# Start-up of a planned attention layer: the second group's input loaded first, one query buffer cleared at once, the first group's normalisation given to VectorE

## The chip, the cores and the metric

The program runs on one core of a Trainium2 chip. Its metric is device time in microseconds, the median of several executions. A profiled execution adds a trace: every instruction of the five engines (TensorE, shown as PE with its weight loads as PEld; VectorE as DVE; ScalarE as ACT; GpSimd as POOL; SyncE as SP, which here only issues transfers) with start, duration and what it waited for.

## The reference, cut to what matters

Two transformer layers over x of 2 x 2048 x 256. Each computes a layer norm, then adds an attention and a mixture of experts of the same normalised x. Layer 0, which the change is about, is:

```python
xn = layernorm(x)                                  # 4096 rows of 256
q = rope((xn @ Wqa @ Wqb)  -> 16 heads of 16)
k, v = (xn @ Wkva @ Wkvb)  -> 4 heads of 16, k = rope(k)
w = softmax(causal(q k^T / 4)); out = (w v) @ Wout + bout
logits = xn @ Wg                                   # 8 experts, top 2, capacity 1280
y = sum over the 2 experts of gate * (gelu(a) * g) @ W_out,  [a, g] = xn @ W_in
x = x + out + y
```

Layer 1 has an attention with 32 fixed keys and sparsemax, and a second mixture of experts. Nothing of it is edited.

## The kernel before, in words

**Tiles.** The 4096 rows are eight *groups* of 512 rows (4 tiles of 128), four per batch. A group is fetched into one of two buffers `xg`, normalised in place, turned (`normed`, tile `tp`, result `xnT` in a ring of two `xt`), multiplied with the joined low-rank and gate weights (`lows`, tile `lw`, result `low`), and its gate logits are turned back (`logits`, tile `tpl`). From `low` come keys and queries of a 512-row block: `rope_products` (tile `pab`) multiplies twice, VectorE multiplies by the cosine and sine tables `cs_sb`, a sum makes the rotated value, ScalarE rounds it (`rope_high`), a subtraction gives the rest (`rope_low`), and both parts go to DRAM (`kd`, `qd`) and come back spread over partitions into `ks` (5 buffers) and `q` (4 buffers). These buffers must be zero elsewhere: `clean_k` by ScalarE, `clean_q` by GpSimd. The tables come from `cs` products; the values from `make_v` (tile `pv`, weights `wkv16[64:96, 8:12]`).

**Attention.** A unit is one group of four heads over 512 queries, `j`. Its row maxima are found first: `maxima` (tile `s`, then VectorE's maximum `part`), `negate_max`, `flip_max` (`mtT`, `mr`), and `place_max`, which sends the maxima into `q`. Then `score` (tile `sc`, exponential on ScalarE into `es`) and `values` (tile `av`).

**Experts.** After all eight groups' logits, `p_route` chooses and counts (tile `before`), GpSimd scatters 4096 rows twice into `buf` (64 indirect transfers at L734), and six experts of layer 0 (`ext`, `exh`, `exy`) are woven into the rest of the attention.

**Order.** Engines execute in the order written. That order is made while the program is built: a planner holds a time for each engine (`T["PE"]`, `T["V"]` VectorE, `T["A"]` ScalarE, `T["G"]` GpSimd, `T["S"]` SyncE), a list of `jobs` with the time from which each is ready, and picks what TensorE does next by a price among candidates. `later(eng, duration, ready, f, then)` adds a job; `flush()` writes down the jobs that are due. Engine names `VL`, `AV` and `AVL` leave a choice: `VL` is VectorE, but held back while GpSimd's time is ahead; `AV` is ScalarE or VectorE, whichever is free sooner; `AVL` is the same with GpSimd's time counted against VectorE. Where the planner sees a gap on TensorE in the early part, `fill()` writes a product that is not used (tile `idle`). `prep` holds the groups, tables, keys, queries and values in order of their due progress; `GRP0` and `GRPN` set those of the groups, `T.update(...)` the engines' starting times, and the argument of `landed` the time at which a group's x is taken to be there. All of these are numbers of the plan, not of the chip. `pin` keeps an instruction at its place in the program.

**Names and lines.** The transfers of the start are L366 to L381, `clean_q` L358, called at L382 and L383; a group's fetch is `fetch` (L411), its normalisation `layernorm_steps` (L205 and L206 statistics, L213 to L217 roots, L224 to L233 Newton steps on VectorE or L228 to L236 on GpSimd, L240 the normalised tile by ScalarE, L242 by VectorE); products are recorded under L336, turns under L339, SyncE's transfers under L345, the cast of turned tiles under L425, table copies L409, `low` copies L441, the rotation's product L458, its sum L1014, its rounding L465, its rest L472, clearing of keys L363.

Of the kernel before, what the change touches and what calls it, by code (L numbers as in the profile page):

```python
# [11 lines left out]
F32 = mybir.dt.float32  # L12
# [11 lines left out]
P = 128  # L24
# [125 lines left out]
def moe_transformer_kernel(  # L150
# [142 lines left out]
    with ExitStack() as actx:  # L293
# [38 lines left out]
        def pin(ins):  # L332
            return tc.keep_in_program_order(ins)
# [23 lines left out]
        def clean_q(i):  # L357
            pin(G.memset(qsl[i].bitcast(F32), 0.0))  # L358
# [14 lines left out]
        pin(A.dma_start(wa_sb[:, :, 0:96], wa.rearrange("(c p) m -> p c m", p=P)))  # L373
        pin(A.dma_start(wa_sb[:, :, 96:96 + NE], wg.rearrange("(c p) m -> p c m", p=P)))
        raw = [agx[rows, c0:c1].rearrange("p (v c) -> p v c", c=16) for rows, c0, c1 in ((slice(0, 64), 1024, 1536), (slice(64, 96), 1024, 1152))]
        pin(SP.dma_start(raw[1], wkvb[:, 0:256].rearrange("k (v c) -> k v c", c=32)[..., 0:16]))
        pin(SP.dma_start(raw[0].rearrange("p (v t) c -> p v t c", v=2), wqb.rearrange("k v t (g c) -> k v (t g) c", g=4)[..., 0:16]))
        pin(SP.dma_start(wkv16[64:96, 8:12], wkvb[:, 256:320].rearrange("k (g c) -> k g c", c=16)))
        for h in range(2):
            pin(A.dma_start(trif[64 * h:64 * h + 64], cst[:, C_TRI:C_TRI + P].rearrange("(r p) m -> p r m", p=64)))  # L380
        pin(A.dma_start(cst_sb, cst))  # L381
        for i in range(3):  # L382
            clean_q(i)  # L383
        pin(G.memset(identh, 0.0))
        for h in range(2):
            for r in range(2):
# [22 lines left out]
            pin(A.copy(cs_sb[:, :, 512 * blk:512 * blk + 512], ps))  # L409

        def fetch(grp):  # L411
            if grp == 0:
                return
            st[grp]["x"] = xgp.tile([P, 4, E], F32, tag="xg", name="xg")
            for i in range(0, 4, 2):
                sdma(st[grp]["x"][:, i:i + 2], xv[:, 4 * grp + i:4 * grp + i + 2])
# [48 lines left out]
            pin(A.copy(hi, tt[:, 0]))  # L465
            return hi

        def rope_low(tt, r, hi):
            n = tt.shape[0]
            at = 2048 + 512 * r  # L470
            lo = scr[:n, at:at + 512].bitcast(F32R)
            pin(G.tensor_tensor(lo, tt[:, 0], hi.bitcast(F32), ALU.subtract))  # L472
            return lo

        kss, qs, vas = {}, {}, {}
# [376 lines left out]
        def flush():  # L852
            now, done = T["PE"], False
            for job in sorted(jobs, key=lambda z: z[:2]):
                rank, _, eng, dur, ready, f, then = job
                if ready > now or (eng == "S" and T["S"] > now + ISSUE):
                    continue
                if eng in ("VL", "AVL"):
                    held = T["G"]
                    if eng == "VL":  # L860
                        eng = "V"
                        if held > now + 300 and now < ready + 3000:
                            continue
                    else:
                        eng = "A" if T["A"] + 70 <= max(T["V"], held) else "V"
                        if T[eng] > now + 300:
                            continue
                        dur, g = dur[eng == "V"], f
                        f = lambda: g(eng)
                    if eng == "V":  # L870
                        ready = max(ready, held)
                elif eng == "AV":
                    eng = "A" if T["A"] <= T["V"] else "V"
                    if T[eng] > now + 300:
                        continue
                    dur, g = dur[eng == "V"], f
                    f = lambda: g(eng)
                elif eng == "V" and T["V"] > now + 300 and now < ready + 5000:
                    continue
                if eng in "AG" and rank > 1 and T[eng] > now:  # L880
                    continue
                jobs.remove(job)
                moved[0] = 0
                f()
                end = on(eng, dur, ready)
                if eng == "S":
                    end = max(end + LAND, shift(moved[0], end))
                if then:
                    then(end)
                done = True  # L890
            return done
# [52 lines left out]
        def start_fetch(grp):  # L944
            i = take(xg)
            st[grp]["xg"] = i

            def landed(t):
                x_ = st[grp]["x"]
                steps = layernorm_steps(atp, x_, mean_sb[:, 4 * grp:4 * grp + 4], rstd_sb[:, 4 * grp:4 * grp + 4], x_, pin, V if grp < 2 else G)  # L950
                first = 0 if grp == 0 else 1
                costs = [500] * 4 + [600, 1900 if grp < 2 else 3900] + [350] * 4

                def go(k, t):
                    if k == len(steps):
                        at["x", grp] = t
                        later("S", ISSUE, t + 1500, lambda: keep_rows(grp), lambda t: x_done(grp, t), 2)
                    else:
                        if k < 6:
                            later("G" if k == 5 and grp > 1 else "VL" if k == 4 else "V", costs[k], t, steps[k],  # L960
                                  lambda t: go(k + 1, t if 3 < k < 6 and grp > 1 else t - HOP), first)
                        else:
                            later("AVL", (510, 350), t, steps[k], lambda t: go(k + 1, t - HOP), first)
                go(0, t)
            if grp == 0:
                return landed(4300)
            later("S", 2 * ISSUE, 0, lambda: fetch(grp), landed, 2)

        def p_normed(grp):
# [29 lines left out]
        def rope(n, products, done):  # L999
# [6 lines left out]
            def summed(t):  # L1006
                def high(t):
                    def low_(t):
                        at[key] = t
                        done(box, 1, t)  # L1010
                    done(box, 0, t)
                    later("G", 1270, t, lambda: box.update(lo=rope_low(box["tt"], box["r"], box["hi"])), low_, 0)
                later("A", 610, t, lambda: box.update(hi=rope_high(box["tt"], box["r"])), high, 0)
            later("G", 1270, free2[-1], lambda: pin(G.tensor_tensor(box["tt"][:, 0], box["tt"][:, 0], box["tt"][:, 1], ALU.add)),  # L1014
                  summed, 0)

        def both(key, f):

# [86 lines left out]
        for s, j in enumerate(order):  # L1105
            b, qb = j // 16, j // 4 % 4
            first_use.setdefault(("k", b, qb), s)
            first_use.setdefault(("q", j // 2), s)
        LEAD, MOST, EXB, SWX, RUN, ALONE, JOIN, IDLE, GAIN, GRP0, GRPN, QK0, QKN, FILL, TAIL = 2.5, 20.0, 243.0, 215.8, 2, 62.2, 125.5, 72.4, 5092.0, 15.0, 5.5, 36.4, 2.7, 136.0, 11.8
        tab, made = set(), set()  # L1110
        natural = []

# [16 lines left out]
        for s, j in enumerate(order):  # L1129
# [4 lines left out]
                n_qk += 1  # L1134
            grp = 4 * b + qb
            if 0 < grp < 2:
                add_group(grp, d)

            def load_tab(qb=qb):
                cs16["ring", qb] = take(xt)  # L1140
# [291 lines left out]
                    p_project(bq, i0)  # L1432
                yield t - now + late, t, go

        T.update(S=3000, A=3600, G=8500, V=2500)
        prefetch()
        prefetch()

# [1 line left out]
        pin(G.tensor_scalar(zero[:, E:E + 1], meta[:, 0, 0, 0:1], float(NT), None, ALU.add))  # L1440
        for i in range(NKS):
            later("A", 2560, 2000 + 5000 * i, lambda i=i: clean_k(i), None, 2)
        for i in range(3, NQS):
            later("G", 2000, 30000, lambda i=i: clean_q(i), None, 2)
        later("S", 9 * ISSUE, 40000, load_out_weights, None, 2)
        later("S", ISSUE, 48000, lambda: sdma(x1[NT:NT + P], zero[:, 0:E]), None, 2)
        for grp in range(8):
# [1170 lines left out]
```

## Time and profile before

| what | value |
|---|---|
| runs shown | 1947.78 us median (1944.43 to 1949.24, 3 runs) |
| profiled execution | 1942.78 us, span of its trace 1941.0 us |
| busy in the span | PE 1868.6, DVE 1237.6, ACT 1023.5, POOL 667.2 us |
| first maxima product (`s`) | starts at 46.38 us |
| first score (`sc`) | 64.86 us |
| experts counted (`before`) | 217.39 us |
| first expert turn (`ext`) | 426.0 us |
| granted TensorE clock | 0.984 in the mean |

The times of the last rows but one are starts in the trace, counted from the span's start. The profiled execution is 5.0 us shorter than the median of the runs, so sums made in the trace are carried to the median as differences.

### The profile page before, as it was taken

Reading aid. Unit: us, or ns where it says so; the run is one execution under the profiler, and the core shown is the slowest. Engines: PE = TensorE matmul, PEld = TensorE weight load, DVE = VectorE, ACT = ScalarE, POOL = GpSimd, SP = SyncE. Lnnn points to the kernel's source line nnn. Section 1 sums busy time; section 2 is a strip of 40 time slices with the busy share of each in tenths; the row PEclk is TensorE's granted clock in tenths of the full one; section 3 lists DMA queues with packets and bytes.
Section 4 is the critical chain, followed back from the end, with each engine's and each line's share of the span. In section 5 each row is a group of like instructions: output and inputs, shape, how many; then the busy total and the mean of one; then the engine's idle time right before and its main releaser. Section 6 shows DMA issues by size and latency. Waiting matters only on the chain.

```text
span 1941.0 us, 29444 instructions
## 1 busy us (share of the span) xinstructions
PE 1868.6 (96%) x10804; PEld 1128.9 (58%) x10818; DVE 1237.6 (64%) x2541; ACT 1023.5 (53%) x1915; POOL 667.2 (34%) x857
## 2 busy tenths in 40 slices
PE   9999999999999999999999999999899899999996
PEld 5554444445656656665565566556466355578774
DVE  4775777677666664566666766763122759997275
ACT  5354344565656566666666666666511433344451
POOL 5232467631222222223122212223223018755651
PEclk8998999999999999999999999999999899999999
DMA  5446456530233224433222312210152302255538
GB/s 144 144 145 193 140 175 203 159 92 12 64 70 97 67 47 114 110 70 91 74 56 65 84 45 38 51 29 12 37 111 25 109 17 79 99 177 157 184 123 265
DMA packets 144012, 192.92 MB, mean 99 GB/s; under 512 B 17261, under 2 KB 122227, under 8 KB 143730
## 3 DMA queue, kind: packets, MB, share of 16 engines
q1 hardware_dynamic: 115538, 137.18, 23.4%
q0 software_dynamic: 27072, 53.08, 11.6%
q8 instruction: 89, 1.46, 0.3%
q10 hardware_dynamic: 1248, 0.67, 0.1%
q14 instruction: 65, 0.53, 0.1%
HBM read 102.44 MB, written 95.77 MB: 102 GB/s over the span
## 4 chain that ended last, share of the span: by engine, by line
PE 79%; DVE 8%; ACT 4%; issue 3%; POOL 2%; DMA 2%; SPq 0%; ACTq 0%; DVEq 0%; POOLq 0%
PE sc L336 17%; PE av L336 13%; PE s L336 11%; PE exh L336 9%; PE exy L336 5%; PE gu L142 4%; PE po L142 4%; DVE srt L142 3%; PE acc L142 2%; PE pab L336 2%; PE pz L142 2%; DVE part L548 2%; PE idle L336 2%; PE po L336 2%; ACT es L587 2%
## 5 line engine op out<-in xcount | busy, mean ns | idle before, releaser
L587 ACT ACTIVATE es<-sc 128x512 f32<-128x512 f32 (+3 forms) x1280 | 634.9, 531 | 473.0 <-PE sc L336 445.4
L548 DVE TENSOR_REDUCE part<-s 128x2 f32<-128x1024 f32 (+3 forms) x640 | 649.8, 1058 | 249.9 <-PE s L336 248.4
L336 PE MATMUL sc<-q,ks 128*128 128x512 f32 (+3 forms) x1280 | 527.7, 461 | 11.2 <-ACT es L587 8.6
L336 PEld LDWEIGHTS sc<-q,ks 128*128 128x128 f32 x1280 | 220.5, 190 | 171.2 <-ACT es L587 87.8
L336 PE MATMUL av<-es,va 128*32 128x512 f32 (+3 forms) x2560 | 279.3, 539 | 1.9 <-POOL es L589 1.9
L589 POOL TENSOR_SCALAR_AFFINE_SELECT es<-es 128x256 f32<-128x256 f32 x256 | 106.7, 419 | 452.1 <-ACT es L587 450.7
L336 PE MATMUL s<-ks,q 64*128 64x512 f32 (+3 forms) x1280 | 226.4, 423 | 7.4 <-DVE part L548 3.6
L336 PEld LDWEIGHTS s<-ks,q 64*128 64x128 f32 x1280 | 101.6, 186 | 168.9 <-DVE part L548 69.0
L336 PEld LDWEIGHTS av<-es,va 128*32 128x32 f32 x2560 | 64.3, 109 | 117.1 <-issue 98.7
L809 POOL DMA_INDIRECT x<-low,tox x54 | 85.2, 1578 | 136.0 <-issue 37.7
L785 POOL TENSOR_TENSOR agx<-agx 128x1024 f32<-128x1024 f32 (+1 forms) x24 | 52.3, 2180 | 221.0 <-ACT agx L781 221.0
L336 PE MATMUL exh<-cs_sb,low 128*128 128x256 f32 (+1 forms) x480 | 120.7, 360 | 0.0
L336 PE MATMUL exh<-cs_sb 128*128 128x256 f32 (+1 forms) x480 | 120.1, 360 | 0.0
L142 POOL DMA_INDIRECT buf<-xn,slot x64 | 82.7, 1291 | 99.6 <-DVE cmp L142 80.3
L777 DVE COPY agx<-exh 128x512 f32<-128x512 f32 (+1 forms) x91 | 58.5, 643 | 89.7 <-PE exh L336 88.0
L142 POOL DMA_INDIRECT oe<-xn,to x72 | 78.1, 1085 | 46.9 <-ACT xn L142 29.6
L336 PEld LDWEIGHTS exh<-cs_sb 128*128 128x128 f32 x480 | 84.8, 190 | 11.8 <-ACT agx L777 0.3
L336 PEld LDWEIGHTS exh<-cs_sb,low 128*128 128x128 f32 x480 | 84.3, 189 | 12.5 <-issue 0.4
L336 PE MATMUL idle<-ones 128*128 128x256 bf16 (+2 forms) x506 | 82.6, 289 | 1.2 <-POOL ones L184 1.2
L142 DVE TENSOR_TENSOR srt<-srt 128x512 f32<-128x512 f32 (+6 forms) x104 | 75.6, 768 | 3.4 <-ACT srt L142 1.3
L734 POOL DMA_INDIRECT buf<-xsr,idx_sb x64 | 63.6, 993 | 24.1 <-issue 9.1
L142 PE MATMUL gu<-xg,xn 128*128 128x256 f32 x288 | 66.3, 382 | 0.2
(321 smaller groups left out, 2517.5 us busy)
## 6 DMA issues: line engine op xcount, KB each, us to landing
q<-qd SPq DMA_DIRECT2D x128, 128.0 KB
buf<-zero SPq DMA_DIRECT2D x20, 516.0 KB
buf<-zero SPq DMA_DIRECT2D x20, 514.0 KB
xn<-buf SPq DMA_DIRECT2D x18, 514.0 KB
qd<-agx SPq DMA_DIRECT2D x32, 256.0 KB
xsr<-xnd SPq DMA_DIRECT2D x32, 256.0 KB
oe<-zero SPq DMA_DIRECT2D x16, 512.0 KB
xn<-oe SPq DMA_DIRECT2D x16, 512.0 KB
```

The costliest lines, as they stand in the source:

```text
L142: return lambda *a, **k: self.tc.keep_in_program_order(f(*a, **k))
L336: pin(PE.matmul(*args, **kw))
L548: pin(V.tensor_reduce(parts[j][:, i, 2 * pair:2 * pair + 2, kb], sc[:, :, :n], AX.X, ALU.max))
L587: pin(A.activation(es[:, g % 2, :n], sc[:, :n], AF.Exp, scale=0.25))
L589: pin(G.affine_select(es[:, :, 0:P], es[:, :, 0:P], pattern=[[0, 2], [1, P]], compare_op=ALU.is_ge, fill=0.0, base=0, channel_multiplier=-1))
L734: pin(G.indirect_dma_start(ways[(2 * ti + k) % 8], bass.IndirectOffsetOnAxis(ap=idx_sb[:, k, ti:ti + 1], axis=0), xsr[:, ti % 3, k], None, ...
L777: pin((A.copy if eng == "A" else V.tensor_copy)(ag[i % 2][:, :, f, 0:n], exs["ps"][:, :, 0:n]))
L785: pin(eng.tensor_tensor(a, a, g, ALU.mult))
L809: pin(G.indirect_dma_start(x1[:], bass.IndirectOffsetOnAxis(ap=exs["to", i][:, c:c + 1], axis=0), ysx[:, c], None, compute_op=ALU.add))
```

## The change

Group 1's x is loaded by two SyncE transfers right behind the tables, ahead of the key, value and query weights; the value weights move to ScalarE's queue. Only one query buffer is cleared at the start; the three others become GpSimd jobs of the plan. The roots of group 0 go to plain VectorE and its normalised tiles to whichever of ScalarE and VectorE is free sooner. The rotation's sum and rest may go to VectorE when the plan finds GpSimd later by more than `ROPEV`. The plan's starting times, the landing of groups 0 and 1 and the due progress of group 1 are set anew. All later instructions are placed by the same planner from these numbers, so the order of the whole of layer 0 is written anew.

```diff
@@ -373,14 +373,16 @@
         pin(A.dma_start(wa_sb[:, :, 0:96], wa.rearrange("(c p) m -> p c m", p=P)))
         pin(A.dma_start(wa_sb[:, :, 96:96 + NE], wg.rearrange("(c p) m -> p c m", p=P)))
         raw = [agx[rows, c0:c1].rearrange("p (v c) -> p v c", c=16) for rows, c0, c1 in ((slice(0, 64), 1024, 1536), (slice(64, 96), 1024, 1152))]
+        st[1]["x"] = xgp.tile([P, 4, E], F32, tag="xg", name="xg")
+        for i in range(0, 4, 2):
+            pin(SP.dma_start(st[1]["x"][:, i:i + 2], xv[:, 4 + i:4 + i + 2]))
         pin(SP.dma_start(raw[1], wkvb[:, 0:256].rearrange("k (v c) -> k v c", c=32)[..., 0:16]))
         pin(SP.dma_start(raw[0].rearrange("p (v t) c -> p v t c", v=2), wqb.rearrange("k v t (g c) -> k v (t g) c", g=4)[..., 0:16]))
-        pin(SP.dma_start(wkv16[64:96, 8:12], wkvb[:, 256:320].rearrange("k (g c) -> k g c", c=16)))
+        pin(A.dma_start(wkv16[64:96, 8:12], wkvb[:, 256:320].rearrange("k (g c) -> k g c", c=16)))
         for h in range(2):
             pin(A.dma_start(trif[64 * h:64 * h + 64], cst[:, C_TRI:C_TRI + P].rearrange("(r p) m -> p r m", p=64)))
         pin(A.dma_start(cst_sb, cst))
-        for i in range(3):
-            clean_q(i)
+        clean_q(0)
         pin(G.memset(identh, 0.0))
         for h in range(2):
             for r in range(2):
@@ -409,7 +411,7 @@
             pin(A.copy(cs_sb[:, :, 512 * blk:512 * blk + 512], ps))
 
         def fetch(grp):
-            if grp == 0:
+            if grp < 2:
                 return
             st[grp]["x"] = xgp.tile([P, 4, E], F32, tag="xg", name="xg")
             for i in range(0, 4, 2):
@@ -465,11 +467,11 @@
             pin(A.copy(hi, tt[:, 0]))
             return hi
 
-        def rope_low(tt, r, hi):
+        def rope_low(tt, r, hi, eng):
             n = tt.shape[0]
             at = 2048 + 512 * r
             lo = scr[:n, at:at + 512].bitcast(F32R)
-            pin(G.tensor_tensor(lo, tt[:, 0], hi.bitcast(F32), ALU.subtract))
+            pin(eng.tensor_tensor(lo, tt[:, 0], hi.bitcast(F32), ALU.subtract))
             return lo
 
         kss, qs, vas = {}, {}, {}
@@ -855,7 +857,11 @@
                 rank, _, eng, dur, ready, f, then = job
                 if ready > now or (eng == "S" and T["S"] > now + ISSUE):
                     continue
-                if eng in ("VL", "AVL"):
+                if eng == "GV":
+                    late = max(T["G"], ready) + dur[0] > max(T["V"], ready) + dur[1] + ROPEV and T["V"] <= now + 300
+                    eng, dur, g = "V" if late else "G", dur[late], f
+                    f = lambda: g(V if late else G)
+                elif eng in ("VL", "AVL"):
                     held = T["G"]
                     if eng == "VL":
                         eng = "V"
@@ -957,13 +963,15 @@
                         later("S", ISSUE, t + 1500, lambda: keep_rows(grp), lambda t: x_done(grp, t), 2)
                     else:
                         if k < 6:
-                            later("G" if k == 5 and grp > 1 else "VL" if k == 4 else "V", costs[k], t, steps[k],
+                            later("G" if k == 5 and grp > 1 else "VL" if k == 4 and grp else "V", costs[k], t, steps[k],
                                   lambda t: go(k + 1, t if 3 < k < 6 and grp > 1 else t - HOP), first)
                         else:
-                            later("AVL", (510, 350), t, steps[k], lambda t: go(k + 1, t - HOP), first)
+                            later("AVL" if grp else "AV", (510, 350), t, steps[k], lambda t: go(k + 1, t - HOP), first)
                 go(0, t)
             if grp == 0:
-                return landed(4300)
+                return landed(4500)
+            if grp == 1:
+                return landed(7300)
             later("S", 2 * ISSUE, 0, lambda: fetch(grp), landed, 2)
 
         def p_normed(grp):
@@ -1009,10 +1017,10 @@
                         at[key] = t
                         done(box, 1, t)
                     done(box, 0, t)
-                    later("G", 1270, t, lambda: box.update(lo=rope_low(box["tt"], box["r"], box["hi"])), low_, 0)
+                    later("GV", (1270, 680), t, lambda eng: box.update(lo=rope_low(box["tt"], box["r"], box["hi"], eng)), low_, 0)
                 later("A", 610, t, lambda: box.update(hi=rope_high(box["tt"], box["r"])), high, 0)
-            later("G", 1270, free2[-1], lambda: pin(G.tensor_tensor(box["tt"][:, 0], box["tt"][:, 0], box["tt"][:, 1], ALU.add)),
-                  summed, 0)
+            later("GV", (1270, 680), free2[-1],
+                  lambda eng: pin(eng.tensor_tensor(box["tt"][:, 0], box["tt"][:, 0], box["tt"][:, 1], ALU.add)), summed, 0)
 
         def both(key, f):
 
@@ -1106,7 +1114,7 @@
             b, qb = j // 16, j // 4 % 4
             first_use.setdefault(("k", b, qb), s)
             first_use.setdefault(("q", j // 2), s)
-        LEAD, MOST, EXB, SWX, RUN, ALONE, JOIN, IDLE, GAIN, GRP0, GRPN, QK0, QKN, FILL, TAIL = 2.5, 20.0, 243.0, 215.8, 2, 62.2, 125.5, 72.4, 5092.0, 15.0, 5.5, 36.4, 2.7, 136.0, 11.8
+        LEAD, MOST, EXB, SWX, RUN, ALONE, JOIN, IDLE, GAIN, GRP0, GRPN, QK0, QKN, FILL, TAIL, ROPEV = 2.5, 20.0, 243.0, 215.8, 2, 62.2, 125.5, 72.4, 5092.0, 15.0, 5.5, 36.4, 2.7, 136.0, 11.8, 600
         tab, made = set(), set()
         natural = []
 
@@ -1134,7 +1142,7 @@
                 n_qk += 1
             grp = 4 * b + qb
             if 0 < grp < 2:
-                add_group(grp, d)
+                add_group(grp, min(d, GRP0 - 0.01))
 
             def load_tab(qb=qb):
                 cs16["ring", qb] = take(xt)
@@ -1432,7 +1440,7 @@
                     p_project(bq, i0)
                 yield t - now + late, t, go
 
-        T.update(S=3000, A=3600, G=8500, V=2500)
+        T.update(S=6500, A=8000, G=10400, V=2500)
         prefetch()
         prefetch()
 
@@ -1440,8 +1448,8 @@
         pin(G.tensor_scalar(zero[:, E:E + 1], meta[:, 0, 0, 0:1], float(NT), None, ALU.add))
         for i in range(NKS):
             later("A", 2560, 2000 + 5000 * i, lambda i=i: clean_k(i), None, 2)
-        for i in range(3, NQS):
-            later("G", 2000, 30000, lambda i=i: clean_q(i), None, 2)
+        for i in range(1, NQS):
+            later("G", 2000, (0, 14000, 28000, 45000)[i], lambda i=i: clean_q(i), None, 2)
         later("S", 9 * ISSUE, 40000, load_out_weights, None, 2)
         later("S", ISSUE, 48000, lambda: sdma(x1[NT:NT + P], zero[:, 0:E]), None, 2)
         for grp in range(8):
```

## The prediction, made before the changed kernel ran

> **What bounds the kernel now.** I read the stretches of the span first, cut at the first maxima product (46.4 us), the first score (64.9), the count of the experts' rows (217.4), the first expert turn (426) and the end of layer 0 (1404). Columns are the stretch, its length, then busy us (and instructions) of PE, PEld, DVE, ACT and POOL, granted clock, DMA share, GB/s.
>
> ```profile
> 0.00:46.40 46.40, 42.51 (x194) 24.41 (x194) 20.23 (x75) 25.96 (x43) 25.33 (x51) 0.85 0.48 137
> 46.40:64.90 18.50, 16.64 (x164) 10.45 (x163) 13.50 (x25) 3.29 (x6) 5.86 (x17) 1.00 0.61 189
> 64.90:217.40 152.50, 143.06 (x961) 73.98 (x960) 105.60 (x195) 74.51 (x162) 45.96 (x116) 0.94 0.50 154
> 217.40:426.00 208.60, 202.33 (x1240) 96.90 (x1241) 147.33 (x182) 100.26 (x208) 125.64 (x169) 0.98 0.55 164
> 426.00:1404.00 978.00, 963.30 (x6160) 581.91 (x6160) 605.37 (x754) 630.25 (x1144) 233.15 (x311) 1.00 0.25 61
> ```
>
> The same view for the unused products (tile idle) alone says how much of that busy time is filler:
>
> ```profile
> 0.00:46.40 46.40, 18.59 (x128) 0.85 0.48 137
> 46.40:64.90 18.50, 7.80 (x59) 1.00 0.61 189
> 64.90:217.40 152.50, 24.45 (x144) 0.94 0.50 154
> 217.40:426.00 208.60, 31.75 (x177) 0.98 0.55 164
> 426.00:1404.00 978.00, 0.00 (x0) 1.00 0.25 61
> ```
>
> From 426 us TensorE is the bound: 98% busy, no filler, full clock. Before it, TensorE waits in disguise: 82.6 us of filler, 21.5 us idle, and clock lost. So a start that is earlier counts only if it is still earlier at 426 us, or if more work is done by then. The timeline of VectorE and ScalarE at the start (start, us, instruction, idle before it in brackets) shows the stall that the change aims at:
>
> ```profile
> 6.80 0.18 DVE L206 BATCH_NORM_AGGREGATE mv<-st 128x2 f32<-128x6 f32 x1
> 10.09 0.43 DVE L205 BATCH_NORM_STATS2 st<-xg 128x6 f32<-128x256 f32 x1 [3.10 <-DMA xg<-in_x_dram]
> 10.64 0.30 DVE L213 TENSOR_SCALAR sv<-mv 128x4 f32<-128x4 f32 x1
> 11.36 2.56 ACT L363 ACTIVATE ks<-ones,onecol 128x512 fp32r<-128x512 f32 x4
> 13.82 2.06 ACT L240 ACTIVATE xg<-xg,sd,rstd_sb 128x256 f32<-128x256 f32 x4
> ```
>
> Group 0's statistics end at 6.98, but a statistic of group 1 stands ahead of group 0's roots and waits until 10.09 for an x issued at 6.72.
>
> **The change part by part.** The order of the built programs shows what the planner made of it. Group 0's roots now follow its statistics, one statistic of group 1 comes before the Newton steps, and VectorE normalises all four tiles. From the rows: roots 10.64 to 11.49, 0.85; statistic 0.6; Newton 11.46 to 13.38, 1.9; four tiles at 0.37 (0.73 for two in the row at 20.16), 1.5. So 7.0 + 4.9 = 11.9 us instead of 15.9. Turns, copies and low products follow as now: low's copy ended at 20.2 and now does at about 16.4. One risk is group 1's x: its first half is issued at about 2.3, and x took 3.4 us to land (6.72 to 10.09), so 5.7, before VectorE needs it at 7.8.
>
> Queues: SyncE's weights move past two transfers of 0.5 us, and its fifth issue waited until 4.75 for the first x, so the query weights leave at about 6.4 instead of 4.75 and land, at the at most 3.75 us that they took, by 10.2. GpSimd, freed of two memsets of 1.76, waits there; its first late consumer is the query product at 18.6, so this costs nothing, and 1 us per us only if it were 8 us later. ScalarE's one more issue (about 0.5) delays its table load from 6.58 to 7.1; the tables' copy has until 18. The memsets come back behind the first queries, in slack.
>
> Then keys: the product at 16.6, rotated by 19.8, summed by 21.1. ScalarE has two key buffers (5.1 us) queued ahead of the rounding, so it starts at 21.7, not 26.08. The queries' rounding, which stood at 32.88 behind group 1's low copy, comes after a third key buffer at about 25.0; the rest on GpSimd at 25.6 to 26.9. SyncE: key loads from 27.5, query loads from 30, the first query buffer landed at about 34.5 (43.5 before). Now group 1 is late: its Newton steps stand behind the values' copy on VectorE, its four tiles alternate with group 2's statistics, all done at 28.2 (23.8 before), its turn, copies and low products end at 31.8 to 33.5. The order puts these and 31 fillers ahead of the first maxima product; at 0.112 to 0.19 each (57 took 6.40, 18 took 3.44), it starts at 35.3 to 39.4. I take 37.7: **-8.7**.
>
> What is late next: before, the second block's tables, keys, queries and values (1.98 + 1.93 + 1.98 + 1.1 = 7.0 us) were done by then; now they stand between the first maxima and the first score, with two of VectorE's 1.22 us. The stretch there had 7.8 us of filler, 42 remain of 59, and one query pair (1.98) and four maxima products fall behind the first score. I get it at 58: -7, so **+1.7** given back, and **+1** for the work that is now behind it (between 0 and 3.3: beside filler, or all on TensorE).
>
> The whole order of layer 0 moves. Products are the same, fillers 505 for 506 in all: 196 instead of 143 from the first score to the count, 132 instead of 177 from there to the first turn. By that turn 4 more maxima products, 3 more scores and 4 more value products are done: with the page's 226.4 us for 1280, 527.7 for 1280, 279.3 for 1280 pairs, 0.7 + 1.2 + 0.9 = 2.8 us; work done earlier and paid earlier, **0**. TensorE changes its kind of product more often: full to maxima 67 times instead of 47 before the first turn, 135 for 123 after it. A score before a maxima product took 510 ns start to start, before an expert's 339: 0.17 x 32 = 5.4, the value switches about even. While fillers show slack half of it hides: **+2.5** (0 to 5.4).
>
> Clock: 0.94 of 152.5 us loses 9.2, 0.98 of 208.6 loses 4.2. The first loss lies where the order adds 53 fillers. I take a third of 13.4, **-4.5** (0 to -9).
>
> Sum: -8.7 + 1.7 + 1 + 0 + 2.5 - 4.5 = -8.0, so 1934.8 for the profiled execution's 1942.8, and 1939.8 on the median of 1947.8, since the rest of the program is untouched.
>
> Two rules against it. From 36.20 to 46.40 PE was busy for all of 10.20 us, and the granted clock was 0.67; in it are products of 32 and 64 rows (3.06 us for the query product that took 1.98 at 22.16). The Trainium skill, "TensorE: Matmul & The Clock Gate", Part 1, says that the clock is halved after an idle window of about 3.4 us and that busyness keeps it; by that, fillers put where nothing idles would win no clock, the term of -4.5 would be 0 and the sum -3.5. The row differs from the rule: busy time at few rows also lost the clock, so I keep the row.
> And VectorE's norms run beside GpSimd's copies of the weights. The Trainium skill, "SBUF — State Buffer", "Who interferes with whom", says a VectorE instruction in a two-port mode locks GpSimd out for its whole length; an estimate by it would be four tiles, 1.5 us of GpSimd's slack and no change of the sum. No row of before shows the two together.
>
> **The rivals.** *Washed out:* the fillers and switches are paid in full and the clock stays as it is: -8.7 + 1.7 + 3.3 + 5.4 = +1.7 at worst, -3 in the middle, 1942 to 1949. For it: 82.6 us of filler hides any early gain, and group 1 itself is later. *Slower:* the count comes later and the scatter does not catch up. To the count, 53 more fillers at 0.17 (24.45 / 144) are 9.0, more maxima, scores and values 12 x 0.18 + 7 x 0.41 + 12 x 0.22 = 7.7 plus four value-weight products 1.1 and the 2.4 put behind the first score, 20.2; less the 7, the count is at 230.6. If GpSimd's 64 dispatches then need the 208.6 us that they took, the first turn is at 439, 13 late; 2.8 us of work done ahead leaves **+10**, 1958. It decides if the stretch from count to first turn stays above 201 us. Against: GpSimd was busy for 125.6 of the 208.6, so the order of TensorE, with 45 fillers fewer (8 us) and less work, sets the pace. *All kept:* the early 7 us reach the first turn and most clock comes back: -12 to -16, 1932 to 1936. That the change doesn't do what it says is excluded for the start by the order.
>
> **How the numbers follow.** A run pair tells about 0.3%, 5.8 us, from no change. Forecast and all kept, below 1942: 0.52 (0.42 and 0.10). Washed out, within 5.8: 0.22. Slower: 0.26, mostly 1954 to 1962. The range leaves out half of *all kept* and about half of *slower*: 1930 to 1957. The forecast's own range is 1934 to 1942.
>
> **What would show it.** Right: no wait of VectorE for x after 6.98; norms done by 12.5; low's copy by 17; the first maxima product at 35 to 40; the first score at 56 to 60; a count within 10 us of 217; the first turn at or before 423; a clock above 0.95 between score and count. Wrong: a first score after 62, GpSimd's copy of the query weights behind 16 us, or a first turn after 429.

## The result, and the profile after

The changed kernel took 1953.81 us in the median (1946.25 to 1960.38, 22 runs), the kernel before on the same chip 1947.55 (1942.27 to 1958.21, 22 runs). The ratio is 1.0028, with an interval from 1.0016 to 1.0039: slower by 0.28%, where 8 us less had been forecast. The profiled execution took 1954.7 us, span 1953.0, mean granted clock 0.976 (before 1942.78, 1941.0 and 0.984).

The stretches of the changed kernel, cut at the same events as before (the last one at layer 1's first expert output product, tile `py`); columns as in the prediction:

```profile
0.00:40.90 40.90, 34.19 (x181) 21.35 (x181) 21.16 (x71) 20.50 (x33) 20.95 (x47) 0.87 0.51 143
40.90:71.80 30.90, 29.97 (x151) 16.46 (x150) 13.63 (x26) 1.90 (x3) 3.35 (x3) 0.56 0.18 49
71.80:240.50 168.70, 159.90 (x1089) 84.11 (x1087) 119.54 (x220) 77.04 (x170) 52.73 (x135) 0.95 0.53 163
240.50:445.60 205.10, 200.21 (x1163) 93.43 (x1160) 147.26 (x177) 99.04 (x203) 124.80 (x166) 0.94 0.53 160
445.60:1432.00 986.40, 969.81 (x6189) 591.27 (x6188) 602.98 (x756) 640.05 (x1156) 233.64 (x314) 1.00 0.26 63
```

The unused products (tile `idle`) alone:

```profile
0.00:40.90 40.90, 18.80 (x135) 0.87 0.51 143
40.90:71.80 30.90, 9.65 (x43) 0.56 0.18 49
71.80:240.50 168.70, 31.99 (x196) 0.95 0.53 163
240.50:445.60 205.10, 24.24 (x132) 0.94 0.53 160
```

The start is shorter by 5.5 us, the stretch to the first score longer by 12.4 (30.9 for 18.5), the one to the count by 16.2; then 3.5, 6.0 and 1.6 come back. That adds up to the 12.0 us between the two spans. The medians are only 6.3 us apart, since the profiled execution of the kernel before was 4.8 us faster than its median and that of the changed kernel 0.9 slower. The second line is the odd one: PE was busy for 29.97 of 30.90 us, with fewer fillers than before (43 for 59), and its clock was 0.56. The fourth is lower too, at 0.94, where the kernel before had 0.98.

The timeline of VectorE at the start shows the part that worked:

```profile
6.84 0.18 DVE L206 BATCH_NORM_AGGREGATE mv<-st 128x2 f32<-128x6 f32 x1
7.05 0.17 DVE L213 TENSOR_SCALAR sv<-mv 128x4 f32<-128x4 f32 x1
...
10.06 1.37 DVE L242 TENSOR_SCALAR xg<-xg,mean_sb,rstd_sb 128x256 f32<-128x256 f32 x4
```

No wait for x stands between the statistics and the roots, and the four tiles are normalised at 11.43 us (before 15.9). Inside the odd stretch, the timeline of TensorE reads (start, us):

```profile
50.48 3.78 PE L336 MATMUL cs<-cs,sel 16*128 16x512 f32 x4
...
59.28 1.48 PE L336 MATMUL idle<-ones 64*128 64x256 bf16 x6
60.69 3.67 PE L336 MATMUL pab<-low,wkv 32*64 32x512 f32 x4
64.29 3.78 PE L336 MATMUL pab<-low,wq 64*128 64x512 f32 x4
68.00 1.96 PE L336 MATMUL pv<-wkv,low 32*128 32x64 f32 x8
```

The products with few rows are the tables (`cs`), keys, queries (both `pab`) and values (`pv`) of the second block. Before, they ran ahead of the first maxima product, with fillers of 128 rows behind them:

```profile
34.36 1.98 PE L336 MATMUL cs<-cs,sel 16*128 16x512 f32 x4
36.27 1.93 PE L336 MATMUL pab<-low,wkv 32*64 32x512 f32 x4
38.13 3.06 PE L336 MATMUL pab<-low,wq 64*128 64x512 f32 x4
41.12 1.96 PE L336 MATMUL pv<-wkv,low 32*128 32x64 f32 x8
43.01 3.44 PE L336 MATMUL idle<-ones 128*128 128x256 bf16 x18
```

Tables and keys take nearly twice as long now. Queries and values had run at half clock in part or in whole before, too; the first block's took 1.98 and 1.10 us at full clock. The number ahead of the star is the rows of a product: 16, 32 and 64 of 128, and nearly all fillers between them have 64 (40 of 43). The clock of the stretch, in the same columns as above:

```profile
40.90:44.90 4.00, 3.27 (x44) 2.21 (x44) 2.15 (x5) 0.00 (x0) 0.00 (x0) 0.99 0.91 256
44.90:75.60 30.70, 30.50 (x123) 16.47 (x121) 13.23 (x23) 3.60 (x6) 3.90 (x4) 0.50 0.12 33
```

For 30.7 us TensorE was 99% busy and ran at half clock. It began at 44.9, ahead of the tables: only maxima products and fillers of 64 rows had run since 41.4.

### The profile page after: what moved, and what is told of

It reads as the page before. It is cut to its first block, busy times and chain, and to the rows that moved or that the text cites. A ratio compares the mean times of both kernels' runs of the same rounds, so it can differ in the third digit from the quotient of the medians.

```text
span 1953.0 us, 29440 instructions
## 1 busy us (share of the span) xinstructions
PE 1881.9 (96%) x10803; PEld 1140.1 (58%) x10817; DVE 1245.5 (64%) x2549; ACT 1023.4 (52%) x1909; POOL 663.2 (34%) x855
## 5 line engine op out<-in xcount | busy, mean ns | idle before, releaser
L336 PE MATMUL s<-ks,q 64*128 64x512 f32 (+3 forms) x1280 | 231.4, 428 | 7.6 <-DVE part L550 2.1
L779 DVE COPY agx<-exh 128x512 f32<-128x512 f32 (+1 forms) x86 | 54.4, 632 | 81.2 <-PE exh L336 75.2
L142 PE MATMUL gu<-xg,xn 128*128 128x256 f32 x288 | 66.4, 382 | 0.2
```

Source lines behind the costliest of these rows:

```text
L142: return lambda *a, **k: self.tc.keep_in_program_order(f(*a, **k))
L336: pin(PE.matmul(*args, **kw))
L779: pin((A.copy if eng == "A" else V.tensor_copy)(ag[i % 2][:, :, f, 0:n], exs["ps"][:, :, 0:n]))
```

## The experiments

Three theories were put against each other. *Clock:* the earlier first maxima leaves products of few rows alone with fillers of 64 rows, and the clock falls to half. *Count stage:* the order written anew is itself longer, fillers and kinds of product included. *Start:* the earlier start is not worth what it seems.

Two readings go through all of them. First, every run lists its granted clock, and within one kernel the time follows it: over 22 runs of the changed kernel from 0.971 to 0.981 the correlation is -0.91 and the slope -15 us per 0.01, over 29 of the kernel before -0.94 and -14. So "at clock 0.980" means below the time that the line fitted to a kernel's runs gives for that clock: 1948.6 to 1949.3 for the kernel before in the three series beside the experiments (mean clock 0.9797 to 0.9809), 1948.3 for the changed one (mean clock 0.9768). The three series of one kernel differ by 0.7 us in this reading, and it is weaker where a kernel's runs lie away from 0.980. Secondly, these are the events in the one profiled execution of each (us):

| kernel | first maxima | first score | count | first turn | `py` |
|---|---|---|---|---|---|
| before | 46.4 | 64.9 | 217.4 | 426.0 | 1418.5 |
| changed | 40.9 | 71.8 | 240.5 | 445.6 | 1432.1 |
| e1_full_rows | 39.2 | 64.0 | 230.3 | 436.4 | 1422.9 |
| e4_full_rows_early | 41.9 | 66.7 | 233.6 | 438.7 | 1425.3 |
| e3_before_half_rows | 46.4 | 73.0 | 228.4 | 439.0 | 1433.2 |
| e2_before_full_rows | 49.1 | 67.5 | 218.5 | 428.7 | 1421.4 |
| f1_start_alone | 46.2 | 64.6 | 217.9 | 428.5 | 1422.7 |

One execution is not the kernel. Up to the first maxima the order and the fillers of the changed kernel, e1, e4 and f2 (below) are the same, and that product came at 40.9, 39.2, 41.9 and 39.4; in the kernel before, e2 and f3 it came at 46.4, 49.1 and 47.8. So an event of the start differs by up to 2.7 us between executions of the same order.

**Rows of the fillers.** e1 gives every filler 128 rows, e4 only those ahead of the first score; nothing else of the changed kernel's order moves. e3 does the opposite to the kernel before, with 64 rows for the fillers ahead of the first score, and e2 is the control, the kernel before with 128 rows throughout.

```diff
-            rows, cols = (64 if model["mode"] == "s" else P), ...
+            rows, cols = P, ...                                                  # e1 (changed), e2 (before)
+            rows, cols = (64 if model["mode"] == "s" and pos["sc"] else P), ...  # e4 (changed)
+            rows, cols = (64 if model["mode"] == "s" or (("v", 0, 1) in at and not pos["sc"]) else P), ...  # e3 (before)
```

> The changed kernel, in the same order of instructions; only the unused filler products among maxima products use all 128 rows of TensorE instead of 64. Theory clock (the loss is the granted clock, at half from 44.9 to 75.6 us because only products of 16, 32 and 64 rows were there): no half clock longer than 7 us before the first score, first score at 57 to 63 us instead of 71.8, and the time 8 to 14 us below the changed kernel's 1953.8, at 1940 to 1946. Theory order (the second block's tables, keys and queries now stand between the first maxima and the first score, and 53 more fillers follow): the first score stays after 67 us and the time within 4 us of 1953.8.

> As the run before, but only the fillers ahead of the first score use all rows; later ones stay at 64. Theory clock: first score at 57 to 63 us, and most of the gain of the run before, 6 to 12 us below 1953.8. Theory order: no gain.

> The kernel before, in the same order of instructions; the 18 fillers right ahead of the first maxima product and the other fillers up to the first score use 64 rows instead of 128. Theory clock: the half clock that ended at 45.7 us goes on into the maxima stage, the first score comes at 71 to 80 us instead of 64.9, and the time is 6 to 15 us above 1947.6. Theory order: first score within 2 us of 64.9 and no difference in time.

> The kernel before, in the same order; all fillers use 128 rows. Control for the first run. Theory clock: its maxima stage already had the full clock, so the first score stays at 63 to 66 us; some of the later half clocks (158 to 172 us, 203, 237 to 244, 291) may go, so 0 to 5 us below 1947.6. Theory order: no difference, and the gain of the first run, if any, is the same here.

The groups of TensorE from the first maxima to the first score (busy us, mean ns), e1:

```profile
L336 PE MATMUL idle<-ones 128*128 128x256 bf16 x43 | 7.7, 326 | 0.0
L336 PE MATMUL pab<-low,wq 64*128 64x512 f32 x4 | 2.4, 710 | 0.0
L336 PE MATMUL pab<-low,wkv 32*64 32x512 f32 x4 | 1.9, 600 | 0.0
```

and the changed kernel:

```profile
L336 PE MATMUL idle<-ones 64*128 64x256 bf16 (+1 forms) x43 | 9.9, 392 | 0.0
L336 PE MATMUL pab<-low,wq 64*128 64x512 f32 x4 | 3.8, 1097 | 0.0
L336 PE MATMUL pab<-low,wkv 32*64 32x512 f32 x4 | 3.7, 1069 | 0.0
```

The same 43 fillers and 8 products: with 128 rows in the fillers the keys are back at 1.9 us, and the first score comes at 64.0 (e1) and 66.7 (e4) instead of 71.8. Two more profiled executions have the changed kernel's fillers and order up to the first score, f2 in full and f4 with two GpSimd instructions exchanged, and both have the stretch:

```profile
42.90:73.60 30.70, 30.50 (x133) 16.38 (x133) 13.32 (x23) 3.50 (x6) 4.00 (x4) 0.50 0.14 38
```

```profile
46.60:70.50 23.90, 23.69 (x93) 11.79 (x93) 9.43 (x20) 3.60 (x6) 4.21 (x5) 0.50 0.13 36
```

e3 makes it in the kernel before:

```profile
46.40:73.00 26.60, 26.60 (x168) 18.02 (x165) 14.56 (x26) 3.29 (x6) 6.09 (x17) 0.50 0.53 166
```

26.6 us at half clock without a gap, where the same products took 18.5 at full clock. The kernel before had fillers of 64 rows in that place, too:

```profile
L336 PE MATMUL idle<-ones 64*128 64x256 bf16 x55 | 7.3, 269 | 0.0
```

With these 55 its clock stayed at 1.00 from 46.4 to 64.9. What e3 took from it are the 128 rows of the 18 fillers at 43.01, right ahead of the first maxima, and of 4 later ones: before, the half clock of 38.9 to 45.7 ended with the 18, and in e3 it went on. So 64 rows did not bring the clock back, and 128 did; where the clock was full, 64 rows held it in the kernel before and did not in the changed one. What parts these last two is not shown.

In time, e3 was at 1.0059 (1.0038 to 1.0080) to the kernel before, e4 at 1.0003 (0.9982 to 1.0024), e1 at 1.0019 (0.9999 to 1.0039), e2 at 1.0014 (0.9997 to 1.0032). So rows of fillers cost 0.6% when they are taken from the kernel before; given back to the changed one ahead of the first score (e4), its difference of 0.28% is gone. But e1 has the same fillers up to there and gave back only 0.09%. e1's interval does not part it from the changed kernel, and e4's only just; the mean clock of their runs rose from 0.9768 to 0.9780 and 0.9792. Both stayed under what the clock theory had asked for, a first score at 57 to 63 and medians 8 to 14 and 6 to 12 us lower: they were 0.9 and 4.2 us lower. e2 shows no gain from full rows where the clock was not lost; its first maxima came 2.7 us late behind a start whose clock was 0.79 instead of 0.85, with the same fillers.

**The start by itself.** f1 loads group 1's x early and gives VectorE group 0's four tiles in the kernel before, with the numbers of the plan as they were, so that the order of TensorE and GpSimd stays. e5 does the opposite: 40 fillers ahead of group 0's turn.

```diff
+        st[1]["x"] = xgp.tile([P, 4, E], F32, tag="xg", name="xg")             # f1
+        for i in range(0, 4, 2):
+            pin(SP.dma_start(st[1]["x"][:, i:i + 2], xv[:, 4 + i:4 + i + 2]))
-            if grp == 0:
+            if grp < 2:
+                moved[0] += 4 * P * 4 * E
...
-  later("AVL", (510, 350), t, steps[k], ...
+  later("AVL", (510, 350), t, (lambda eng, k=k: [f("V") for f in (steps[6:] if k == 6 else [])] if grp == 0 else steps[k](eng)), ...
...
+            if grp == 0:                                                        # e5
+                for _ in range(40):
+                    product()
```

> The kernel before with the start of the change and without its new order: group 1's x is loaded right behind the tables, and VectorE normalises group 0's four tiles right behind the Newton steps; every other instruction stands in the order of the kernel before, since the plan's numbers are as they were. No stall of VectorE for x, group 0's tiles at about 12 us instead of 15.9, low's copy ended at 17 to 18 instead of 20.2. Theory pass-through (the start is worth its length; the change lost it by its new order and by the clock): first maxima 2 to 3 us earlier, 1.5 to 3 us faster at equal granted clock. Theory washed out: within 1 us at equal clock.

> The kernel before, in the same order, with 40 more unused full-row products ahead of the first group's turn: the first group's turn, and all behind it, starts 3 to 4.5 us later (40 products at 0.112 us, less the half us that TensorE waited there). It measures what a microsecond at the start is worth at the end. Theory pass-through (a start that is earlier by x ends earlier by x, and what the change lost it lost later): 3 to 4.5 us slower at equal granted clock. Theory washed out (fillers and waits before 426 us absorb the start): 0 to 1 us at equal clock.

In f1 the keys' product of the first block started at 18.59 us instead of 20.33, and the first maxima product at 46.16 instead of 46.38. The clock of the two executions says where the rest of the 1.7 us went; f1 first, then the kernel before:

```profile
22.00:32.00 10.00, 9.22 (x28) 5.25 (x27) 4.59 (x15) 1.55 (x4) 4.57 (x4) 0.50 0.30 86
```

```profile
22.00:32.00 10.00, 9.22 (x30) 4.88 (x30) 5.80 (x16) 3.28 (x7) 4.68 (x4) 0.66 0.31 90
```

The half-clock stretch that was there already was 10.2 us instead of 6.8. That this is f1's doing is not shown: f3, the same as the kernel before up to its first score, had 10.2 us there as well (23.5 to 33.7) and its first maxima at 47.8, 1.65 us behind f1's. f1's ratio is 0.9996 (0.9981 to 1.0012), a tie; at clock 0.980 it is 0.6 us faster, where 1.5 to 3 had been expected of a start that passes through. e5 moved the low products by 2.6 us and cost 3.0 at clock 0.980, ratio 1.0023 (1.0003 to 1.0043), although its profiled execution, without the half clock between 22 and 32 us, had its first maxima only 0.5 late. So a late start was paid, and an early one was repaid by little or nothing; why is not shown.

**The order.** e7 gives only the roots and tiles of group 0 to VectorE in the kernel before, and lets the planner write the order anew; e8 takes just this out of the changed kernel; e6 is e4 with group 1 added behind the second tables in the plan.

```diff
-  later("G" if k == 5 and grp > 1 else "VL" if k == 4 else "V", ...
+  later("G" if k == 5 and grp > 1 else "VL" if k == 4 and grp else "V", ...   # e7; undone in e8
-  later("AVL", (510, 350), ...
+  later("AVL" if grp else "AV", (510, 350), ...                               # e7; undone in e8
...
+            if grp < 2:                                                       # e6
+                add_group(grp, min(d, GRP0 - 0.01))
```

> The kernel before with one part of the change: group 0's roots go to plain VectorE and its normalised tiles to whichever of ScalarE and VectorE is free; loads, clearing and the plan's times are as before. Group 0's tiles are done at 12 to 12.5 us instead of 15.9. Theory pass-through: first maxima product 2 to 4 us earlier than 46.4 and 2 to 4 us faster at equal clock. Theory washed out: within 1.5 us at equal clock. Fillers ahead of the first expert turn are 492 instead of 506, which speaks for up to 2 us more.

> The changed kernel without that part: loads, clearing, the plan's times and the rotation's choice are as in the change, the roots and tiles of group 0 as before. Its order has the second block's products ahead of the first maxima again, and 542 fillers ahead of the first expert turn. Theory order: without the displaced products the first score comes at 56 to 63 us and the time at equal clock is 1 to 5 us below the kernel before. Theory washed out: within 2 us of it, or up to 5 us slower by its 36 more fillers (0.17 us each).

> The changed kernel with full-row fillers ahead of the first score, and with one line of the plan moved: the second block's tables stand ahead of group 1's turn, so that they, its keys, queries and values are done before the first maxima, as in the kernel before. The order after it is written anew. Theory order (these products, moved between the first maxima and the first score, gave back the early start): first score at 56 to 62 us instead of 66.7 with the same fillers, and 2 to 7 us faster than the kernel before at equal granted clock. Theory washed out: the first score may be early, but the time at equal clock stays within 2 us of the kernel before, since 42 more fillers stand ahead of the first expert turn.

None of the three did what was expected at its place. e7's tiles were done at 15.4 us, not at 12 to 12.5, and its first maxima came at 46.9. It counted at 200.6 us, but lost the gain by its first turn at 429.7, at a clock of 0.92 between; that is its fastest run, at clock 0.981, and the mean of its runs is 0.9728. Its ratio is 1.0061 (1.0044 to 1.0078); the 2.0 us by which it is faster at clock 0.980 rest on that one run, since the others lie at 0.970 to 0.972. e8 was at 1.0095 (1.0076 to 1.0115), its first score at 71.5 (56 to 63 expected) behind 27.4 us of half clock. e6 had its first score at 66.4 (56 to 62 expected) and was at 1.0087 (1.0070 to 1.0105), 14.7 us slower than the kernel before at equal clock; from e4 it differs by one moved line of the plan. What one such edit does through the order is larger than what it does at its place.

**The fillers.** f2 and f3 leave out the fillers between the first score and the choice of experts, 190 in the changed kernel and 132 in the kernel before.

```diff
+            if pos["sc"] and "choose" not in at:
+                return
```

> The changed kernel in the same order, without the 190 unused products between the first score and the choice of experts; the kernel has them to keep the clock. Theory stream (TensorE's own list of products, fillers too, sets the pace from the first score to the first expert turn, so that the fillers cost what they take): that stretch is 15 to 25 us shorter than 168.7 us at the full clock, if the clock holds; with a clock lost to half for 30 us more it gains nothing. Theory slack (fillers only stand where TensorE would wait): the stretch keeps its length within 4 us, with 20 us more idle time of TensorE.

> The same for the kernel before: without its 132 unused products between the first score and the choice of experts. Theory stream: the stretch of 152.5 us is 10 to 18 us shorter at the full clock. Theory slack: within 4 us, with as much more idle time. If the difference between the two kernels in this stretch (16.2 us) shrinks by the difference of their fillers, about 6 to 8 us, the 53 more fillers were part of what the change gave back.

First score to count, f2 and then f3:

```profile
70.90:245.80 174.90, 156.76 (x899) 75.18 (x897) 119.23 (x220) 77.33 (x170) 52.63 (x135) 0.83 0.51 158
```

```profile
66.30:222.50 156.20, 142.10 (x829) 66.83 (x829) 106.02 (x195) 73.64 (x161) 45.71 (x114) 0.86 0.47 148
```

The clock fell from 0.95 and 0.94 to 0.83 and 0.86, and both stretches grew, from 168.7 and 152.5 us; the 16.2 us between them became 18.7, where a difference smaller by 6 to 8 was to show that the added fillers were part of the loss. Carried on to clock 0.980, which none of their runs reached (0.962 to 0.974 and 0.974 to 0.978), the fitted lines give 1941.4 and 1941.5, about 7 us less than with fillers: by this estimate the fillers do cost time. The mean clock falls to 0.9666 in f2, ratio 1.0056 (1.0035 to 1.0077), and to 0.9758 in f3, ratio 1.0000 (0.9983 to 1.0018). So the 190 fillers together are no loss: without them the changed kernel is slower still. The 53 added ones were not tried alone.

**Group 1.** Its four tiles were forecast for 28.2 us and were done at 31.25. The timeline of VectorE shows small operations drawn out:

```profile
19.70 1.27 DVE L214 TENSOR_SCALAR sd<-sv 128x4 int32<-128x4 int32 x1
21.01 0.95 DVE L215 TENSOR_SCALAR sv<-sv 128x4 f32<-128x4 f32 x1
...
22.70 1.12 DVE L224 TENSOR_TENSOR sd<-rstd_sb 128x4 f32<-128x4 f32 x1
23.85 2.42 DVE L225 TENSOR_TENSOR sd<-sd,sv 128x4 f32<-128x4 f32 x1
26.30 0.16 DVE L226 SCALAR_TENSOR_TENSOR rstd_sb<-sd,rstd_sb 128x4 f32<-128x4 f32 x1
```

and that of GpSimd what ran beside them, the rotation's sums (L1023) and rests (L474), and a clearing (L489):

```profile
19.68 1.26 POOL L1023 TENSOR_TENSOR agx<-agx 64x512 f32<-64x512 f32 x1 [4.24 <-DVE sv L213]
20.89 1.04 POOL L489 MEMSET va<- 128x1104 f32 x1
...
22.53 1.27 POOL L1023 TENSOR_TENSOR agx<-agx 128x512 f32<-128x512 f32 x1 [0.60 <-DVE agx L460]
23.75 2.49 POOL L474 TENSOR_TENSOR agx<-agx 64x512 fp32r<-64x512 f32 x2
```

f4 has GpSimd clear the first two rests instead of computing them (the low parts of the first block's keys and queries are left out).

```diff
+            if ropes["n"] <= 2:
+                pin(eng.memset(lo.bitcast(F32), 0.0))
+                return lo
```

> The changed kernel in the same order; for the first block, GpSimd clears the rounding's rest of keys and queries instead of computing it, so their low parts are left out. In the changed kernel VectorE's Newton steps of group 1, 0.16 us each elsewhere, took up to 2.42 us while GpSimd computed these rests. Theory lock (the two engines hold each other up): the Newton steps take 0.13 to 0.2 us each, and group 1's tiles are done at 27 to 29 us instead of 31.25. Theory chance (VectorE waited for something else): the long steps stay.

VectorE and then GpSimd in f4:

```profile
24.44 0.29 DVE L224 TENSOR_TENSOR sd<-rstd_sb 128x4 f32<-128x4 f32 x1
24.76 0.16 DVE L225 TENSOR_TENSOR sd<-sd,sv 128x4 f32<-128x4 f32 x1
```

```profile
24.65 0.98 POOL L475 MEMSET agx<- 64x512 f32 x2
```

The same two steps took 0.29 us, at the end of a sum, and 0.16, beside a memset. Group 1's tiles were done at 29.9 (27 to 29 expected) although the values' copy came 1.7 later than in the changed kernel, at 24.1. The nearer comparison is f2: its copy came at 24.1 too, its L225 took 2.42, and its tiles were done at 32.6, 2.7 later than f4's. f4's first maxima product started at 38.0, f2's at 39.4. L225 took 2.41 to 2.43 us in e1, e4 and e6 as well. The sums were left in, and L214 still took 1.27 beside one. The Trainium skill, "SBUF — State Buffer", "Who interferes with whom", says that a VectorE instruction with two inputs in SBUF contends with a GpSimd instruction that reads SBUF and not with one that only writes it. These two traces agree with it on L225, 2.42 us against 0.16. L214 and L215 have one input only, so this sentence does not cover them: beside a sum and beside the clearing of `va` they took 1.27 and 0.95 us, 0.17 each in group 0.

## Why the prediction was wrong

**The start held up to low's copy.** No wait of VectorE after the statistics, tiles done at 11.43 for 11.9 forecast, SyncE's weights out at 6.14 (6.4), low's copy ended at 16.2 (16.4). GpSimd copied the query weights at 11.49, within its slack.

**The first maxima product was off by 3.2 us.** It came at 40.87 instead of 37.7, outside the 35.3 to 39.4 given. The step that failed is group 1's tiles, 31.25 for 28.2. The prediction had weighed one direction of the engines' interference, VectorE holding up GpSimd, and found it free; the other direction cost this group about 3 us. Term -8.7, measured -5.5 in this pair; the means of the four executions of the one order (40.35) and the three of the other (47.75) differ by -7.4.

**Given back: +1.7 forecast.** The first score was to come 20.3 us after the first maxima product; it came after 30.9, so +12.4 instead of +1.7. The prediction priced the second block's products at 1.98, 1.93, 1.98 and 1.1 us, 7.0 in all, which are prices of full clock (the last two the first block's). They took 1.98, 1.93, 3.06 and 1.96 before and 13.2 in all here. e4 and e1, with the same order, took 24.8 at clocks of 0.76 and 0.77. e4 had 11.7 us of half clock in it; at full clock half of that, 5.8, goes, an estimate of 19.0. So by this estimate the work was counted rightly and its rate was not.

**The clock is the step that failed and decided.** The term was -4.5, between 0 and -9, and it had no other side. It was to come out of the stages from the first score to the first turn, where the kernel before lost 9.2 and 4.2 us (the missing share of the clock times the length). The profiled changed kernel lost 8.4 (0.95 of 168.7) and 12.3 (0.94 of 205.1) there, and 13.6 (0.56 of 30.9) between the first maxima and the first score, where the kernel before lost nothing and the sum had no term for it. The prediction itself had read that TensorE lost its clock from 36.20 to 46.40 while it was busy throughout with products of few rows, and that these products were about to move between the first maxima and the first score, where the fillers have 64 rows. It drew the wrong consequence: it counted 53 more fillers as cover. The runs' mean clock went from about 0.980 to 0.9768: 0.003 to 0.004 at 15 us per 0.01 is 4.4 to 6.2 us lost, against 4.5 gained in the forecast. At equal clock the changed kernel is 0.3 to 1.0 us faster than the kernel before, which is no difference. So the clock is what makes it slower, by this comparison. That half clock ahead of the first score costs time, e3 shows; that taking it from the changed kernel gives the time back, e4 shows at the edge of its interval, and e1 less. All three profiled executions with the changed kernel's fillers there have the stretch (30.7, 30.7 and 23.9 us); the runs that were not profiled could not be seen. How much of the 0.28% is this stretch stays open. The other loss, between count and first turn, is in e1, e4 and f4 as well (clocks 0.93, 0.94 and 0.94), not in f2 (0.97) and not in the kernel before, e2, e3, f1 and f3 (0.97 to 0.98). No experiment was aimed at it.

The rule against the term was dropped by halves. The Trainium skill, "TensorE: Matmul & The Clock Gate", Part 1, has the clock depend on how busy TensorE has lately been. Here it was 0.50 over 30.70 us with 30.50 busy, and e1 changed only the rows of the fillers: the measurement decides, and how many rows were busy counted as well, though not alone: the kernel before kept 1.00 among products and fillers of 64 rows. Applied to the new order, the row that the prediction kept would have asked for a loss.

**The rest of the sum, at equal clock.** The rival *slower* gave a count at 230.6 and a first turn at 439. With part of the early clock given back, e1 had 230.3 and 436.4, e4 233.6 and 438.7, and the stretch between, 205 to 206 us, stayed above the 201 from which that rival decides. Part of this is luck. The stretch from first score to count was 166 to 169 us, where the rival's 20.2 on 152.5 are 172.7, and the first scores were 6 to 9 us behind its 58: two misses that cancel. That GpSimd's dispatches set the pace from count to first turn is not shown either: TensorE was busy for 200.21 of the 205.10 us, and f2, with the same products there and a clock of 0.97, took 201.3. And its +10 did not follow, since more work was done by then than the 2.8 us counted: from the first turn to `py` the changed kernel, e1 and e4 took about 986.5 us, the kernel before 992.5. What remained at equal clock is near the middle of *washed out*, -3 forecast (its terms add up to -3.5) for -0.3 to -1.0. Of the +2.5 for changes of kind no run gives a measure of its own; in the traces the changes from a score straight to a maxima product rose from 33 to 56 up to the first turn, but those from a value product fell from 39 to 22. And where the order's 15 us between e6 and e4 lie was not followed up. None of the cases had a clock that gets worse.

Of the signs named, no wait for x, tiles by 12.5 and low's copy by 17 came true; the first maxima (40.9), the first score (71.8), the count (23 late) and the first turn (445.6) did not; the clock between score and count was 0.95, hardly above the 0.94 of before. A first score after 62 and a first turn after 429 had been named as signs of failure.

No kernel tried was faster than the one before: f1 (0.9996), f3 (1.0000) and e4 (1.0003) are ties.

## What to carry to other kernels

Where a profile shows TensorE busy and its clock low at once, list the rows of its products there, and when a change moves such products, price the clock to both sides. Count the rows of fillers, not only their number: here 43 fillers of 128 rows kept part of the clock (0.76 and 0.77) where 43 of mostly 64 rows lost it (0.56), and in the other kernel 128 rows ended a half-clock stretch that 64 rows let go on. Where a planner rewrites the order, a gain at the start is worth what is left of it where TensorE becomes the bound, and a run's granted clock has to be read before its time. Profile more than one execution before a difference of 2 or 3 us in an event is put down to an edit.

## What was not expected of the hardware

- TensorE ran at half clock for 30.7 us while it was busy for 30.5 of them, and for 41.0 us (39.2 to 80.2, busy for 40.2) in e3. The same 64 rows held the full clock for 18.5 us in the kernel before.
- The scatter of the runs is largely that of the clock: 1946.25 to 1960.38 us in the changed kernel, at clocks from 0.981 down to 0.971, correlation -0.91.
- A VectorE step on 128 x 4 numbers took 2.42 us beside two subtractions on GpSimd, and 0.16 beside a memset; another, with one input, took 0.95 beside a memset.
- Where half clock falls differs between executions of one order: between 22 and 34 us the kernel before had 6.8 us of it, and f3, the same up to there, 10.2.
